# Attention and output projection on one core: stores, copies, scalings and operand loads moved where the first part ends

## The chip, the cores and the metric

The kernel runs on one core of a Trainium2 chip, in one launch. The metric is the device time of a run in microseconds (us). The engines have their own instruction queues and meet by semaphores: TensorE (PE: matrix products, transposes), VectorE (DVE), ScalarE (ACT), GpSimd (POOL), and SyncE (SP), which in this kernel issues every DMA. An instruction that has to wait holds up everything behind it in its own queue, SP's DMAs included.

## The reference

A transformer block in float32 over 8 sequences (b) of 512 rows and 1024 columns; 16 heads of 64.

```python
x = hidden                                   # [8, 512, 1024]
h = layernorm(x)
q, k, v = h @ Wq, h @ Wk, h @ Wv             # 16 heads of 64
q, k = rotary(q), rotary(k)                  # pairs of columns turned by cos, sin
s = where(causal, q @ k.T, -1e9) / sqrt(64)
attn = softmax(s) @ v
x = x + layernorm(attn @ Wo)
h = layernorm(x)
y = h @ weight.T + bias                      # plus a LoRA product chosen per sequence
x = x + layernorm(y + lora)
```

## The kernel before, in words

**Products.** All large products (values, queries and keys, output projection `wo`, feed-forward `wf`) are done by a two-level scheme in the manner of Strassen and Winograd: seven products in place of eight, and again seven in each. Operands are sums and differences called S1 to S4 and T1 to T4 beside the blocks L11 ... R22. So a unit of work is 7 groups (P1 to P7) of 7 products, 49 "ticks" (`N2`), and one tick on PE is one product: for queries and keys 8 matrix instructions, for the projection 4.

**The clock of the program.** There is no planner with costs. The order of the work is written by hand: `at(tick, fn)` puts a function on a tick, and `run(tick, filler)` first emits what is marked "pe" on that tick, then the tick's product, then everything else on it in the order in which it was registered. Each engine's queue, SP's too, has its instructions in this order and takes them strictly one after the other. A number such as 57 in the code is therefore not a time but a place in the queues.

**First part.** Values of all sequences come first (not touched here). Then eight units u = 0 to 7 (`UQ` = 8) each make queries and keys of half of the heads for two sequences. A product's two operands, `ls` and `xs`, are loaded eight products ahead into a ring of nine (`load_slot`). The results stand in tiles A, B, D, E, F; `plan_unit` says on which ticks the sums are made and the rotation (`rotate`, six steps) is done: for each half j of the tokens and half q of the heads, steps 0 to 3 are multiplications on VectorE, step 4 two additions on GpSimd or VectorE, and step 5 stores the rotated rows to the `qk` tiles by 8 DMAs, from SBUF to SBUF (lines 681 to 689).

**Attention** over unit u is done beside the products of unit u + 1, in eight pairs (`Pair`: two heads of one sequence; pairs 2i and 2i + 1 share the heads i). A pair handles its four blocks of 128 rows as (0, 1), (2) and (3):

- `scores`: PE makes s in PSUM (line 742). One tile of s exists; the next scores wait until VectorE has read it.
- `exps`: VectorE adds the mask and takes the smallest value (line 763), ScalarE exponentiates (line 773) and sums.
- `scale`: VectorE's reciprocal (line 781), then ScalarE multiplies each row (line 784).
- `transpose`: PE turns the blocks (line 798) into PSUM tiles `ptp`, of which two exist.
- `keep`: the turned blocks are copied to `pT` in SBUF (lines 808, 809 and 812), the first head (j = 0) by ScalarE and the second (j = 1) by VectorE; in the last unit both copies of block 2 are VectorE's.
- `values`: PE multiplies by v into `po` (line 818); `store` copies that to `ops` (VectorE, line 833), and after the last pair of a sequence `sum` makes the differences on GpSimd and stores them to `attn` in DRAM (lines 846, 848 and 849).

The pairs of unit 6 run beside unit 7, one in 5 ticks. Those of unit 7 have no unit beside them ("alone"): they are planned 6 ticks apart from tick 51 of unit 7, and run on into ticks 2 to 59 of a further unit "8" that has no products. From its tick 20 on PE fills with the first 21 products of the output projection of sequence 0 (`first_product`; groups P1, P2, P4), one in three ticks and later one a tick.

**Second part.** The projection of sequences 0 to 7 and then their feed-forward, 49 products each, go on from the 22nd product (`AHEAD` = 21; from here ticks count from 0 at sequence 0, so sequence 1 begins at tick 49). `plan_right(q, base)` plans for item q the loads of R11, R21, R12 and R22 from `attn` and GpSimd's differences T1 = R12 - R11, T2 = R22 - T1, T4 = R21 - T2, T3 = R22 - R12 (`sum_right`, line 275). Item q's operands are put in buffers that item q - 1 has done with: `next_roles` says which; R12 goes where T4 was, R22 where T1 was. Left operands `wo_S2` and `wo_S4` are loaded by `load_sums` (line 242) into memory that the `qk` tiles and the mask leave when the last scores have been read (`rows_qk`, closed at tick 49). For q = 1 the loads are on ticks 21 (R12), 29 (R22), 30 (R11) and 33 (R21).

Of the kernel before, what the change touches and what calls it, by code (L numbers as in the profile page):

```python
# [13 lines left out]
ALU = mybir.AluOpType  # L14
# [118 lines left out]
def sandwich_kernel(  # L133
# [15 lines left out]
    nc = tc.nc  # L149
# [44 lines left out]
    def at(tick, fn, kind=None):  # L194
        events[tick].append((kind, fn) if kind else fn)
# [48 lines left out]
    def open_right(pool, q, n):  # L244
        RX[q, n] = pool.tile([P, 7, 2, P], F32, tag=f"g{role[n]}", name=f"{n}_{q}")

    def load_right(pool, q, n):

        g, h = int(n[1]) - 1, int(n[2]) - 1
        open_right(pool, q, n)  # L250
        if q < B:
            nc.sync.dma_start(out=RX[q, n], in_=attn[q][:, g, h])
            return
        src = x1t[q - B]
        nc.sync.dma_start(
            out=RX[q, n][:, 0:4].rearrange("p (t k) c n -> p t (k c n)", t=2),
            in_=src[:, 2 * h : 2 * h + 2, ts(g, NH), :].rearrange("p t k n -> p t (k n)"),
        )
# [6 lines left out]
    def sum_right(pool, q, n, eng, part=slice(0, 3)):  # L265

        x, y = {"T1": ("R12", "R11"), "T2": ("R22", "T1"), "T4": ("R21", "T2"), "T3": ("R22", "R12")}[n]
        if (q, n) in RX:
            pass
        elif n == "T3":  # L270
            RX[q, n] = RX[q, "R12"]
        else:
            open_right(pool, q, n)
        for c in (slice(0, 2), slice(2, 4), slice(4, 7))[part]:
            eng.tensor_tensor(RX[q, n][:, c], RX[q, x][:, c], RX[q, y][:, c], op=ALU.subtract)  # L275
# [77 lines left out]
    def combine(q, out, x, y, eng):  # L353
        for j in (ALL,) if eng is nc.vector else (0, 1):
            eng.tensor_tensor(C[q, out][:, j], C[q, x][:, j], C[q, y][:, j], op=ALU.add)  # L355
# [181 lines left out]
    for b in range(B):  # L537
        base = b * N2
# [46 lines left out]
    for n in range(8):  # L585
        base = min(n + 1, B - 1) * N2
# [9 lines left out]
    UQ = NG * B // 2  # L596
    PAIRS = B
# [54 lines left out]
    def add_cu(u, out, x, i, eng):  # L652
        o, x = CU[u, out][:, i], CU[u, x][:, i]
        eng.tensor_tensor(o, o, x, op=ALU.add)
# [36 lines left out]
    def plan_unit(u, base):  # L691
        dve, pool = nc.vector, nc.gpsimd
        end = u + 1 == UQ
        for k, eng, out, x in (
            (15, pool, "B", "A"), (22, pool, "A", "D"), (29, pool, "E", "A"), (36, pool, "F", "E"),
        ):
            for i in range(2):
                at(base + k, lambda out=out, x=x, i=i, eng=eng: add_cu(u, out, x, i, eng))
        for k, i, out, x in (
            (43, 0, "A", "D"), (44, 0, "D", "E"), (44, 1, "A", "D"), (45, 1, "D", "E"),  # L700
            (49 if end else 50, 0, "E", "A"), (51 if u else 52, 1, "E", "A"),
        ):
            at(base + k, lambda out=out, x=x, i=i: add_cu(u, out, x, i, dve))

        for j, q, ticks in (
            (0, 0, (38, 39, 40, 41, 42, 44)),
            (0, 1, (41, 42, 45, 46, 47, 49) if end else
                   (42, 46, 47, 48, 49, 51) if u == 0 else (46, 47, 48, 49, 50, 52)),
            (1, 0, (46, 47, 49, 49, 49, 49) if end else
                   (49, 50, 51, 53, 54, 55) if u == 0 else (52, 53, 54, 55, 56, 58)),  # L710
            (1, 1, (52, 53, 54, 55, 56, 58) if end else (57, 58, 59, 60, 61, 63)),
        ):
            eng = dve if (end or u == 0) and j and not q else pool
            for step in range(6):
                at(base + ticks[step], lambda j=j, q=q, s=step, e=eng: rotate(u, j, q, s, e))
# [3 lines left out]
    class Pair:  # L719
# [58 lines left out]
        def scale(self, qbs):  # L778
            for qb in qbs:
                rs = work2["small"].tile([P, 2], F32, tag="rs", name=f"rs_{self.name}_{qb}")  # L780
                nc.vector.reciprocal(rs, self.sm[qb])  # L781
                for j in range(2):
                    v = self.pr[qb][:, j, :]
                    nc.scalar.mul(v, v, rs[:, j : j + 1])  # L784

        def transpose(self, qbs):
            if qbs[0] == 0:
# [14 lines left out]
        def keep(self, qbs):  # L802
            for j in range(2):

                act = j == 0 and (self.u + 1 < UQ or qbs[0] != 2)
                copy = nc.scalar.copy if act else nc.vector.tensor_copy
                if qbs[0] == 0:
                    copy(self.pT[j][:, 0, 0 : 2 * P], self.pt[j][:, 0:2, :])
                    copy(self.pT[j][:, 1, P : 2 * P], self.pt[j][:, 2, :])
                else:  # L810
                    (qb,) = qbs
                    copy(self.pT[j][:, : qb + 1, ts(qb, P)], self.pt[j][:, : qb + 1, :])  # L812
# [121 lines left out]
    for u in range(UQ + 1):  # L934
        for k in () if u in (0, UQ) else (4, 13, 22, 31) if u in (4, 5, 6) else (9, 19, 29):
            base = u * N2 + k
# [17 lines left out]
    AHEAD = 3 * NP  # L954
# [28 lines left out]
    for u in range(UQ + 1):  # L983
        base = u * N2
        if u < UQ:
            plan_unit(u, base)
        if 0 < u < UQ - 1:
            for n in range(PAIRS):
                Pair(u - 1, n).plan(base + 10 + (n * N2 + PAIRS // 2) // PAIRS)
        elif u == UQ - 1:  # L990
            for n in range(PAIRS):
                Pair(u - 1, n).plan(base + 9 + 5 * n, last=11)
            for n in range(PAIRS):
                Pair(u, n).plan(base + 51 + 6 * n, alone=True)
        if u < UQ:
            for n in range(base, base + N2):
                run(n, lambda n=n: unit_product(n))
        else:
            run(base, lambda: cur.drain(NP))
            for k in range(base + 1, base + 10):  # L1000
                run(k, None)
            streams.close()
            chunks.close()

            wop, gp, cl = (tc.alloc_tile_pool(name=name, bufs=1) for name in ("w2", "g2", "cl"))
            env["cl"] = cl
            tl = tc.alloc_tile_pool(name="tl", bufs=1)
            for k, n in (
                (10, "R11"), (10, "L11"), (15, "R12"), (17, "R22"), (21, "L12"), (24, "R21"), (31, "L22"), (42, "S1"),
            ):  # L1010
                if n in ("R11", "R12", "R21", "R22"):
                    at(base + k, lambda n=n: load_right(gp, 0, n))
                else:
                    at(base + k, lambda n=n: load_sums(wop, "wo", n, n))
            for k, n in ((21, "T1"), (26, "T2"), (32, "T4"), (44, "T3")):
                for m in range(3):
                    at(base + k + m, lambda n=n, m=m: sum_right(gp, 0, n, nc.gpsimd, slice(m, m + 1)))
            at(base + 52, lambda: combine(0, "c11", "c11", "A", nc.vector))
            cur, ticks = None, [*range(20, 44, 3), *range(44, 57)]
            for k in range(10, 57):  # L1020
                if k in (54, 56):
                    n = {54: "S2", 56: "S4"}[k]
                    load_sums(wop2, "wo", n, n)
                if k == 49:
                    rows_qk.close()
                    wop2 = tc.alloc_tile_pool(name="w2b", bufs=1)
                    load_sums(wop2, "wo", "S3", "S3")
                if k in ticks:
                    run(base + k, lambda n=ticks.index(k): first_product(n))
                else:  # L1030
                    run(base + k, None)
            cur.drain(NP)
            run_rest()
# [3 lines left out]
    with ExitStack() as a:  # L1037
# [92 lines left out]

        def plan_right(q, base):

            at(max(base + 6, AHEAD), next_roles)
            for n, k in (("R11", 10), ("R21", 17), ("R12", 24), ("R22", 31)):
                if q == 1:
                    k = AHEAD + {"R12": 0, "R22": 8, "R11": 9, "R21": 12}[n]
                at(base + k, lambda n=n: load_right(gp, q, n))
                if q >= B:
                    at(base + k + 4, lambda n=n: sub_right(q, n, nc.gpsimd))
            for n, k in (("T1", 44 if q == 1 else 38), ("T2", 45), ("T4", 52), ("T3", 63)):  # L1140
                eng = nc.vector if q >= B and n in ("T1", "T3") else nc.gpsimd
                for m in range(3):
                    at(
                        base + k + (m if eng is nc.vector else 0),
                        lambda n=n, m=m, eng=eng: sum_right(gp, q, n, eng, slice(m, m + 1)),
                    )
# [76 lines left out]
        for q in range(NQ):  # L1223
            base = q * N2
            if q + 1 < NQ:
                plan_right(q + 1, base)
            if q >= B - 1 and q + 1 < NQ:
                k = 10 if q == B - 1 else 52
# [115 lines left out]
```

## Time and profile before

| | us |
|---|---|
| median of 3 runs | 2520.49 (2519.02 to 2520.89) |
| the profiled execution | 2516.67 |
| its span, first to last instruction | 2514.9 |

| engine | busy, share of the span | instructions |
|---|---|---|
| PE, products | 2399.3 us, 95% | 12192 |
| DVE | 1745.5 us, 69% | 3842 |
| ACT | 1096.5 us, 44% | 2748 |
| POOL | 1508.8 us, 60% | 1127 |

The mean granted clock of TensorE was 0.986 of full. Times inside the profile are in us from the first instruction. A line of the timeline gives start, length, engine (a q behind it: only the issue, as of a DMA), the line of the kernel, the operation, output<-inputs, and in brackets how long the engine had been idle and who ended that. In lists of waits the numbers are total us, how many, and the longest. The page's rows of digits cut the span into 40 slices; a digit is the busy share in tenths. How the stretch from 1540 to 1760 us looks in windows of 20 us:

| window, us | PE busy | DVE busy | ACT busy | POOL busy | clock | what runs |
|---|---|---|---|---|---|---|
| 1540 to 1560 | 19.01 | 17.79 | 10.84 | 6.59 | 1.00 | end of unit 7 |
| 1560 to 1580 | 17.90 | 19.45 | 12.07 | 7.82 | 1.00 | its last products, pairs 5 to 7 of unit 6 |
| 1580 to 1600 | 9.93 | 15.32 | 7.40 | 4.75 | 0.75 | change to the pairs of unit 7 |
| 1600 to 1620 | 16.64 | 13.50 | 16.86 | 9.69 | 0.91 | pairs alone |
| 1640 to 1660 | 16.88 | 14.24 | 16.80 | 12.93 | 1.00 | pairs alone, some projection products |
| 1700 to 1720 | 20.00 | 8.54 | 2.23 | 7.56 | 1.00 | projection of sequence 0 |
| 1720 to 1740 | 15.76 | 11.00 | 5.14 | 17.16 | 0.91 | start of sequence 1 |
| 1740 to 1760 | 19.73 | 16.08 | 12.71 | 15.48 | 1.00 | sequence 1 |

### The profile page before, as it was taken

What the parts mean: (1) busy time and instruction counts of PE and PEld (TensorE: products, weight loads), DVE (VectorE), ACT (ScalarE), POOL (GpSimd) and SP (SyncE); (2) the same over time, 40 slices, a digit from 0 to 9 for tenths busy, and PEclk for the clock granted to TensorE, in tenths of its full rate; (3) what the DMA queues carried; (4) which work ended last, traced back from release to release, by engine and by line L of the source; (5) the groups of instructions that cost most, each with busy time, mean ns of one, the idle gap of its engine ahead of it and who ended that gap; (6) DMA issues with size and microseconds to landing.
All of it is one profiled execution on the core that took longest, in us unless ns stands there. A gap on an engine that the chain in (4) does not pass through costs nothing. (4 is left out here: it accounts for less than half of the span.)

```text
span 2514.9 us, 37116 instructions
## 1 busy us (share of the span) xinstructions
PE 2399.3 (95%) x12192; PEld 1882.0 (75%) x12192; DVE 1745.5 (69%) x3842; ACT 1096.5 (44%) x2748; POOL 1508.8 (60%) x1127
## 2 busy tenths in 40 slices
PE   6999999989999999999999999789999999999997
PEld 4887887777777777777777766457888887888886
DVE  8777766284957759486785957765677776766676
ACT  3323321015555556555555655673444544222222
POOL 3878875225363554637466263336777686887875
PEclk8999999999999999999999999899999999999999
DMA  7687788899899898989989895557656677334434
GB/s 259 205 288 258 246 264 266 285 287 274 265 305 276 257 332 255 328 268 299 322 266 328 255 313 175 183 178 269 207 185 203 218 275 258 133 125 145 141 105 139
DMA packets 415666, 606.02 MB, mean 241 GB/s; under 512 B 127889, under 2 KB 243601, under 8 KB 410866
## 3 DMA queue, kind: packets, MB, share of 16 engines
q1 hardware_dynamic: 415474, 603.64, 73.5%
q8 instruction: 99, 1.62, 0.3%
q14 instruction: 93, 0.76, 0.1%
HBM read 368.65 MB, written 201.33 MB: 227 GB/s over the span
## 5 line engine op out<-in xcount | busy, mean ns | idle before, releaser
L773 ACT ACTIVATE pr<-pr,nm 128x128 f32<-128x128 f32 (+3 forms) x512 | 280.8, 550 | 176.6 <-DVE nm L763 176.4
L784 ACT ACTIVATE pr<-pr,rs 128x128 f32<-128x128 f32 (+3 forms) x512 | 251.8, 551 | 117.7 <-DVE rs L781 117.7
L763 DVE CUSTOM_DVE_ANT_0 pr<-s,mask 128x128 f32<-128x128 f32 (+3 forms) x512 | 224.2, 484 | 40.2 <-PE s L742 37.6
L636 PE MATMUL accb_q_P<-xs,ls 128*128 128x256 f32 x896 | 218.1, 387 | 6.9 <-DVE u_q_P L116 6.9
L636 PE MATMUL accc_q_P<-xs,ls 128*128 128x256 f32 x896 | 218.8, 387 | 4.7 <-DVE E_q L116 4.7
L636 PE MATMUL acca_q_P<-xs,ls 128*128 128x256 f32 x896 | 220.2, 389 | 0.8 <-issue 0.8
L1091 POOL TENSOR_TENSOR c<-c,row 128x512 f32<-128x512 f32 x120 | 160.8, 1360 | 88.2 <-ACT c L415 79.2
L636 PEld LDWEIGHTS acca_q_P<-xs,ls 128*128 128x128 f32 x896 | 167.4, 192 | 52.1 <-issue 22.7
L636 PEld LDWEIGHTS accc_q_P<-xs,ls 128*128 128x128 f32 x896 | 166.3, 191 | 52.7 <-issue 21.7
L636 PEld LDWEIGHTS accb_q_P<-xs,ls 128*128 128x128 f32 x896 | 166.4, 191 | 51.0 <-DVE u_q_P L116 7.7
L742 PE MATMUL s<-qk 64*128 64x128 f32 (+3 forms) x1024 | 192.0, 471 | 7.2 <-DVE nm L763 5.1
L275 POOL TENSOR_TENSOR T<-R,T 128x512 f32<-128x512 f32 (+1 forms) x96 | 173.1, 1829 | 38.1 <-PE accc_P L315 22.7
L798 PE MATMUL ptp<-ident,pr 128*128 128x128 f32 x1280 | 177.6, 277 | 8.4 <-ACT pr L784 7.3
L798 PEld LDWEIGHTS ptp<-ident,pr 128*128 128x128 f32 x1280 | 147.3, 142 | 39.6 <-ACT pr L784 14.2
L562 POOL TENSOR_TENSOR wc_g<-wc_g 128x256 f32<-128x256 f32 (+1 forms) x120 | 122.9, 1042 | 90.1 <-DMA wc_g<-in_wqk_dram 74.7
L818 PE MATMUL po<-pT,v 128*64 128x384 f32 (+3 forms) x1024 | 155.9, 443 | 13.7 <-ACT pT L812 9.8
L677 POOL TENSOR_TENSOR B_q<-B_q,m 128x1024 f32<-128x1024 f32 x16 | 39.7, 2479 | 213.0 <-DVE B_q L675 213.0
L818 PEld LDWEIGHTS po<-pT,v 128*64 128x64 f32 x1024 | 69.7, 138 | 107.2 <-issue 67.0
L337 DVE TENSOR_TENSOR p_P<-accb_P,p_P 128x256 f32<-128x256 f32 x109 | 45.0, 413 | 101.4 <-PE accb_P L315 52.5
L812 DVE COPY pT<-ptp 128x512 f32<-128x512 f32 (+1 forms) x136 | 82.8, 614 | 42.0 <-PE ptp L798 42.0
L337 DVE TENSOR_TENSOR u_P<-accb_P,p_P 128x256 f32<-128x256 f32 x109 | 46.1, 423 | 94.6 <-ACT p_P L342 94.5
L636 PE MATMUL accd_q_P<-xs,ls 128*128 128x256 f32 x448 | 108.9, 386 | 1.1 <-ACT E_q L125 0.7
(1104 smaller groups left out, 5813.0 us busy)
## 6 DMA issues: line engine op xcount, KB each, us to landing
ls<-wqk SPq DMA_DIRECT2D x392, 256.0 KB, 4.9
xs<-xop SPq DMA_DIRECT2D x392, 256.0 KB, 5.1
R<-attn SPq DMA_DIRECT2D x32, 896.0 KB, 5.5
wqk<-wc_g SPq DMA_DIRECT2D x16, 1568.0 KB, 9.4
x<-in_x_dram SPq DMA_DIRECT2D x32, 512.0 KB, 9.7
v<-vd SPq DMA_DIRECT2D x64, 256.0 KB, 4.9
attn<-ops SPq DMA_DIRECT2D x16, 1024.0 KB, 8.3
row<-in_x_dram SPq DMA_DIRECT2D x32, 512.0 KB, 5.7
```

What stands on the lines that cost most here:

```text
L275: eng.tensor_tensor(RX[q, n][:, c], RX[q, x][:, c], RX[q, y][:, c], op=ALU.subtract)
L337: add = lambda out, x, a: nc.vector.tensor_tensor(out, acc[a], x, op=ALU.add)
L562: eng.tensor_tensor(out, x, y, op=op)
L636: nc.tensor.matmul(acc[:, :, w, :], lhsT=ls[:, k, w, :], rhs=xs_[:, :, k, :], start=(first and w == 0 and k == 0), stop=True, skip_group_c ...
L742: nc.tensor.matmul(ps[:, j, at : at + L], lhsT=qT[r, qb], rhs=kT[r, : qb + 1], start=True, stop=True,)
L763: nc.vector.tensor_tensor_reduce(out=v[:, j, :], in0=self.ps[qb][:, j, :], in1=work2["mask"][:, S - L :], scale=-1.0 / HD**0.5, scalar=3.0e38,
L773: nc.scalar.activation(v[:, j, :], v[:, j, :], AF.Exp, bias=nm[:, j : j + 1], scale=-1.0, accum_out=sm[:, j : j + 1],)
L784: nc.scalar.mul(v, v, rs[:, j : j + 1])
L798: nc.tensor.transpose(pt[:, n, :], self.pr[qb][:, j, ts(kb, P)], ident)
L812: copy(self.pT[j][:, : qb + 1, ts(qb, P)], self.pt[j][:, : qb + 1, :])
L818: nc.tensor.matmul(po[j * HD : (j + 1) * HD, kb * P :], lhsT=self.v[:, kb, ts(j, HD)], rhs=self.pT[j][:, kb, kb * P :], start=(kb == 0), s ...
L1091: nc.gpsimd.tensor_tensor(c, c, row[q, t][:, ts(h, HALF)], op=ALU.add)
```

## The change

Four edits, all near the end of the first part.

- (a) In unit 6 alone, step 5 of rotation (1, 0), its 8 row stores, is on tick 57 instead of 58.
- (b) In `keep`, n counts the pairs from the first pair of the last unit. For n = -2, -1 and 0 (the last two pairs of unit 6, the first of unit 7) ScalarE makes all copies to `pT`; elsewhere nothing changes.
- (c) In `scale`, for the last unit, heads i = 1 to 3, blocks 2 and 3 and the second head (j = 1) of the pair, VectorE multiplies in place of ScalarE: 12 instructions.
- (d) `wo` S2 is loaded at tick 51 of unit "8" instead of 54. Sequence 1's change of roles and its loads of R12, R11 and R21, in this order, are on tick 57 of unit "8", ahead of the store of the last pair's differences on tick 59. R22 is on tick 31 of the second part instead of 29, and T1 of sequence 1 on tick 40 instead of 44.

```diff
-                   (49, 50, 51, 53, 54, 55) if u == 0 else (52, 53, 54, 55, 56, 58)),
+                   (49, 50, 51, 53, 54, 55) if u == 0 else (52, 53, 54, 55, 56, 57 if u + 2 == UQ else 58)),
...
                 for j in range(2):
                     v = self.pr[qb][:, j, :]
-                    nc.scalar.mul(v, v, rs[:, j : j + 1])
+                    if self.u + 1 == UQ and self.i and qb > 1 and j:
+                        nc.vector.tensor_scalar(v, v, rs[:, 1:2], None, op0=ALU.mult)
+                    else:
+                        nc.scalar.mul(v, v, rs[:, j : j + 1])
...
-                act = j == 0 and (self.u + 1 < UQ or qbs[0] != 2)
+                n = self.u * PAIRS + 2 * self.i + self.s - (UQ - 1) * PAIRS
+                act = -2 <= n < 1 or j == 0 and (n < 0 or qbs[0] != 2)
                 copy = nc.scalar.copy if act else nc.vector.tensor_copy
...
+            at(base + 57, next_roles)
+            for n in ("R12", "R11", "R21"):
+                at(base + 57, lambda n=n: load_right(gp, 1, n))
             at(base + 52, lambda: combine(0, "c11", "c11", "A", nc.vector))
             cur, ticks = None, [*range(20, 44, 3), *range(44, 57)]
             for k in range(10, 57):
-                if k in (54, 56):
-                    n = {54: "S2", 56: "S4"}[k]
+                if k in (51, 56):
+                    n = {51: "S2", 56: "S4"}[k]
                     load_sums(wop2, "wo", n, n)
...
-            at(max(base + 6, AHEAD), next_roles)
+            if q > 1:
+                at(base + 6, next_roles)
             for n, k in (("R11", 10), ("R21", 17), ("R12", 24), ("R22", 31)):
-                if q == 1:
-                    k = AHEAD + {"R12": 0, "R22": 8, "R11": 9, "R21": 12}[n]
+                if q == 1 and n != "R22":
+                    continue
                 at(base + k, lambda n=n: load_right(gp, q, n))
...
-            for n, k in (("T1", 44 if q == 1 else 38), ("T2", 45), ("T4", 52), ("T3", 63)):
+            for n, k in (("T1", 40 if q == 1 else 38), ("T2", 45), ("T4", 52), ("T3", 63)):
```

## The prediction

> **What bounds the kernel now.** I read the page's 40 slices first, to find where TensorE (PE) is not busy.
>
> ```profile
> span 2514.9 us, 37116 instructions
> PE   6999999989999999999999999789999999999997
> DVE  8777766284957759486785957765677776766676
> PEclk8999999999999999999999999899999999999999
> ```
>
> A slice is 62.9 us. PE is full almost everywhere; the dip in slices 26 and 27 (1572 to 1698 us) is where the query/key units end and attention runs alone. The edited lines all work between 1430 and 1740 us. Next come the waits of PE alone, between 1380 and 1780 us (total us, times, longest):
>
> ```profile
> PE po L818 <- ACT pT L812: 9.8, 7, 2.6
> PE ptp L798 <- ACT pr L784: 5.2, 4, 4.0
> PE po L818 <- DVE pT L812: 3.9, 1, 3.9
> PE accb_P L315 <- DMA R<-attn: 2.3, 1, 2.3
> PE s L742 <- DMA qk<-D_q: 2.0, 2, 1.8
> PE accb_P L315 <- POOL T L275: 1.4, 1, 1.4
> ```
>
> These are three places: the start of unit 7 (`qk<-D_q`), its end (`pT`, `pr`) and the start of the output projection (`R<-attn`, `T`). Everything after them is issued in program order, with PE busy 19.5 to 20 of every 20 us from 1740 on, so a microsecond won here should reach the end. A wait costs more than itself: this is the clock in two of the windows behind such waits (busy us of each engine, then granted clock, DMA share, GB/s).
>
> ```profile
> 1450.00:1452.00 2.00, 2.00 (x6) 1.64 (x5) 0.72 (x4) 1.31 (x4) 2.00 (x2) 0.50 1.03 300
> 1724.00:1726.00 2.00, 2.00 (x6) 1.55 (x5) 0.00 (x0) 0.00 (x0) 2.00 (x3) 0.50 0.17 67
> ```
>
> The timeline gives the causes (start, length, engine; in brackets idle time and who ended it):
>
> ```profile
> 1433.48 3.34 POOL L678 TENSOR_TENSOR D_q<-D_q,m 128x1024 f32<-128x1024 f32 x1
> 1439.74 0.58 SPq L687 DMA_DIRECT2D qk<-E_q  x1
> 1447.60 0.88 PE L742 MATMUL s<-qk 64*128 64x384 f32 x2 [1.82 <-DMA qk<-D_q]
> ...
> 1581.01 0.56 ACT L812 COPY pT<-ptp 128x512 f32<-128x512 f32 x1
> 1584.71 1.22 DVE L678 TENSOR_TENSOR D_q<-D_q,m 128x1024 f32<-128x1024 f32 x1
> 1585.84 0.68 DVE L812 COPY pT<-ptp 128x512 f32<-128x512 f32 x1
> 1586.58 4.02 PE L818 MATMUL po<-pT,v 128*64 128x512 f32 x14 [3.89 <-DVE pT L812]
> ...
> 1644.48 1.49 ACT L784 ACTIVATE pr<-pr,rs 128x128 f32<-128x128 f32 x4 [0.77 <-DVE rs L781]
> 1652.84 0.56 DVE L763 CUSTOM_DVE_ANT_0 pr<-s,mask 128x384 f32<-128x384 f32 x1 [1.03 <-PE s L742]
> ...
> 1707.99 3.13 SPq L252 DMA_DIRECT2D R<-attn  x4
> 1722.84 4.25 POOL L275 TENSOR_TENSOR T<-R,R 128x512 f32<-128x512 f32 x3 [10.06 <-DMA R<-attn]
> ```
>
> First group: GpSimd (POOL) finishes the rows at 1436.8, their stores are issued only from 1439.7. Second: ScalarE (ACT) has copied its half of `pT` by 1581.6, the other half stands behind VectorE's (DVE's) rotation until 1585.8. Third: in the alone phase ACT waits for DVE and DVE for PE. Fourth: the operands R are issued at 1708 and GpSimd waits ten microseconds for them.
>
> **The change part by part**
>
> (a) Rows a step sooner. Unit 6 issues the 8 stores of rotation (1,0) at tick 57 instead of 58. On SP they then stand ahead of one product's two operand loads (issued 1438.2 and 1438.6) and of the 0.61 us issue of a weight chunk (1439.0), and can go when POOL ends, at 1436.8: 2.9 us sooner. The fourth store, which closes the first pair's rows, was issued at 1441.65 and waited on until 1448.6; 2.9 sooner is 1445.7, just where PE ends its product (1445.8). Both waits (1.82 + 0.18) go. The half clock row behind them lasts about 3.4 us (0.50 at 1450 to 1452, 0.65 to 1454), in which PE is busy: 1.7 more. Sum 3.7. SP now waits at these stores for POOL's last 0.4 us or so; behind it stand operand loads issued eight products ahead, some 24 us at 3.03 us a product (1186 us for 392), so nobody waits. The weight chunk comes some 3 us later; POOL, which sums it, idled 8.6 us just before it. Ends: 1.0 (DMA share was 1.02 to 1.03 around 1448 to 1452, and rows land late anyway) and 4.0.
>
> [...]
>
> (b) Copies on ScalarE. For the last two pairs of unit 6 and the first of unit 7 all `pT` copies go to ACT: 4 + 4 + 5 = 13 copies move. Three spots count. One: the 0.54 us copy of 1576.3 leaves DVE, so the rotation ends at 1585.3, not 1585.9. Two: the copy of 1585.84 runs on ACT right behind that of 1581.01, done by 1582.1; PE's values, which with wait and half clock ended at 1590.6, end near 1584.5 (2.37 us at full clock). DVE's next instruction (`ops`, 1590.63) then starts at 1585.3: 5.3 sooner. Three: before the reciprocal of 1597.76, which PE's 3.99 us wait at 1598.72 hangs on, two copies (0.42 + 0.28) and one of 0.55 leave DVE; with overlap 0.9 more. So 6.2 us by 1598. What could be late next is the score matmul on the last unit's (1,0) rows: they landed at 1589.5, 0.5 sooner now, and are wanted by about 1590.8; they hold. Against it: from 1609.1 to 1617.9 ACT has no idle time (3.00 of 3 us busy in both windows from 1608), and the first pair of unit 7 adds two short copies there (0.45 back to back), two of 128x384 (0.8) ahead of the copy that PE's values wait for at 1615.35, and one of 128x512 (0.47) for their second half: 1.7 us back. Net 4.5. The other copies lie where ACT idles (it is busy 12 of 20 us until 1580) and cost nothing; without that they would be 0.4 to 0.6 each. Ends: 0 (ACT takes all back) and 6.8.
>
> (c) Scaling on VectorE. In pairs 2 to 7 (counted from 0) of the last unit one 128x384 and one 128x512 scaling go from ACT to DVE: 12 instructions. The alone phase turns in 11.04 us a pair, and its loop is: scores, DVE reduction, DVE copy of `ops`, two DVE copies, reciprocal, ACT scaling of the small blocks, ACT exponentials, ACT copy, PE values, transposes, scores. The moved scalings are not in it: ACT waits 0.77 for DVE behind one and DVE 1.03 for PE behind the other. So I count 0. The trace of before has no such multiply on DVE; nearest are the 128x512 and 128x384 copies and reductions, 0.69 and 0.55. From below, a 128x2 reciprocal took 0.15. From above, a two-input 128x1024 DVE operation took 1.22 alone and 2.43 beside POOL, so 1.38 for 128x512. I take 0.69 (same size): under the 1.03 of cover that four of the five following reductions have. At 1.38 they cost 4 x 0.35 + 1.0 at the fifth (cover 0.36) = 2.4. As a gain at most 1.
>
> [...]
>
> (d) Operands in another order. S2 is loaded at tick 51, not 54, so ahead of the attention store that SP waits on until 1693.9. The regions it takes are read last by 1680.2 (S3's load, held for the same, is issued then), and DMA idles: 0.54 share from 1680 to 1700. That takes 1.8 MB (4.8 to 5.8 us between landings there) out of a DMA queue that is full from 1694 to 1725. R12, R11 and R21 of the second item are loaded at tick 57, behind PE's last product with the buffer of R12 (1696.4), and no longer behind the last attention store (POOL's sums end 1706.4). By landings: stores 1701, S4 about 1706.5, then 2.2 each for R12, R11, R21: 1713; the last stores 1717.6, R22 (tick 31 in place of 29) 1719.8, before it was 1720.5. R11 landed near 1722.7 and held PE for 2.25, with a half clock row (3.4 us, 1.7 lost): both go. T1, at tick 40, follows the POOL sum ending 1712.8; T2 waits for R22 until 1719.8, and T2 5.25, the c21 sums 2.5 and T4 4.26 end at 1731.8. PE asks for T4 at 1739.03 - 1.44 - 3.95 = 1733.6: that wait of 1.44 goes too, with 1.8 us to spare. Sum 5.4. Behind T2 on POOL stand only sums that now come earlier. Ends: 2.25 (T2 late by another R22) and 6.0 (also the 0.55 at 1735.6).
>
> **Sum.** 3.7 + 4.5 + 0 + 5.4 = 13.6 off the profiled span of 2514.9, so 2501.3. That execution took 2516.67, 1.8 more than its span, and the median of the runs is 3.8 above it: 2501.3 + 1.8 + 3.8 = 2506.9.
>
> **The rivals**
>
> ScalarE takes back what VectorE gives: the 13 copies queue behind exponentials and (b) is worth 0. For it: ACT's full windows from 1608; against: its idle time before 1600. 2511.4.
>
> The half clock stays: other waits in the same 3.4 us keep it. (a) is 2.0, (d) 3.7, sum 10.2: 2510.3. For it: halves of 6.8 us around 1583 and 1597 came with several waits each; against: both single rows follow one wait. [...]
>
> The moves do not do what they say: rows land no sooner on a full DMA (1.0), R22 holds T2 (2.25), copies 0, multiplies cost 2.4: 0.9 gained, 2519.6. For it: shares over 1.0 in both spots; against: POOL is done 2.9 us before the stores.
>
> Slower: the multiplies enter the loop. If each takes the worst DVE row beside POOL, 2.43 for either size, a pair grows by 4.86 - 1.03, six pairs by 23: 2529.9. It decides at 13.6/6 + 1.03 = 3.3 us for both together. For it: POOL runs operand sums for much of 1634 to 1655; against: half the size of the row, and reductions of 0.69 keep 0.69 beside POOL.
>
> **How the numbers follow.** Forecast 0.50, ScalarE 0.20, half clock 0.12, moves void 0.10, slower 0.08. A measurement of this kernel tells about 0.2%, 5 us, from no change. Faster is the first three, 0.82; same 0.10; slower 0.08. The forecast's own range is 2503 to 2510. The range is 2502.5 (every part at its upper end: 4.0 + 6.8 + 1.0 + 6.0 = 17.8) to 2515.5 (5.0 won: (a) whole, (d) at its low end of 2.25, a third of (b), multiplies at 1.38, so 3.7 + 2.25 + 1.5 - 2.4); it leaves out the last two cases, 0.18.
>
> **What would show it.** (a): stores issued near 1437, no PE wait on `qk<-D_q`, clock 1.00 behind it. (b): no `po` wait on DVE; if ACT takes it back, `po` waits on ACT grow at the first pair of unit 7. (c): still about 11 us a pair, multiplies under 1.03. (d): R issued near 1696, no PE wait on `R<-attn` or `T`. Wrong if the multiplies are long, or if a later wait, such as PE's 3.12 us at 2078, grows by what was won.

## The result, and the profile after

The changed kernel took 2504.94 us in the median of 4 runs (2503.67 to 2509.09), the kernel before 2519.76 (2518.46 to 2520.89) in 4 runs beside it: a ratio of 0.9942, interval 0.9929 to 0.9954. It is faster by 14.8 us; 2506.9 was forecast, with 2502.5 to 2515.5 as the range. The profiled execution of the changed kernel took 2504.95, its span 2503.2.

The page's slices first, those of the kernel after:

```profile
span 2503.2 us, 37098 instructions
PE   6999998989999999999999999899999999999997
DVE  8777766284857759586684856775777777766676
PEclk8999999999999999999999999899999999999999
```

The dip of PE was two slices wide, a 7 and an 8; it is now one 8 wide. The waits of PE alone between 1380 and 1780 us, kernel after (total us, times, longest; line numbers are 3 to 4 higher than before, so L822 is the old L818, L816 the old L812 and L801 the old L798):

```profile
PE po L822 <- ACT pT L816: 9.8, 7, 2.6
PE s L742 <- DVE nm L763: 4.8, 8, 1.9
PE ptp L801 <- ACT pr L787: 4.1, 4, 1.6
PE ptp L801 <- ACT pT L813: 1.1, 1, 1.1
PE accb_P L315 <- POOL T L275: 0.6, 1, 0.6
...
PE s L742 <- DMA qk<-D_q: 0.4, 1, 0.4
```

The 3.9 us on VectorE's `pT` and the 2.3 us on `R` are gone, the 2.0 on `qk` have become 0.4, the 1.4 on `T` 0.6, the longest on `pr` has gone from 4.0 to 1.6. The 9.8 us on ScalarE's `pT`, which no part of the change aimed at, are the same to the tenth. The windows behind the old waits, and one that is new, kernel after (columns as in the prediction's fence):

```profile
1450.00:1452.00 2.00, 2.00 (x14) 1.80 (x13) 2.00 (x6) 0.47 (x1) 1.18 (x2) 1.00 0.99 343
...
1618.00:1620.00 2.00, 1.28 (x4) 0.45 (x6) 0.77 (x6) 2.00 (x9) 0.00 (x0) 0.72 1.05 420
1620.00:1622.00 2.00, 2.00 (x8) 0.73 (x6) 0.00 (x0) 0.94 (x4) 0.00 (x0) 0.50 1.02 415
...
1724.00:1726.00 2.00, 2.00 (x11) 1.77 (x10) 0.72 (x4) 1.52 (x2) 2.00 (x3) 1.00 0.74 165
```

At 1450 and 1724 the clock is 1.00 where it was 0.50. At 1618 to 1622 it is 0.72 and 0.50: a half-clock stretch of 3.4 us that the kernel before did not have. The timeline of the kernel after, at the places that the prediction showed:

```profile
1438.76 0.52 SPq L687 DMA_DIRECT2D qk<-E_q  x1
...
1578.61 1.04 ACT L816 COPY pT<-ptp 128x512 f32<-128x512 f32 x2
1579.23 2.85 PE L822 MATMUL po<-pT,v 128*64 128x512 f32 x16 [2.61 <-ACT pT L816]
1583.91 0.68 DVE L837 COPY ops<-po 128x512 f32<-128x512 f32 x1
1585.37 1.05 PE L801 MATMUL ptp<-ident,pr 128*128 128x128 f32 x6 [1.64 <-ACT pr L787]
...
1618.72 4.07 PE L822 MATMUL po<-pT,v 128*64 128x512 f32 x16 [1.21 <-ACT pT L816]
...
1690.79 3.16 SPq L252 DMA_DIRECT2D R<-attn  x3
1714.52 6.33 POOL L275 TENSOR_TENSOR T<-R,T 128x512 f32<-128x512 f32 x3 [3.11 <-DMA R<-attn]
1727.59 1.13 PE L315 MATMUL accb_P<-wo_L,T 128*128 128x256 f32 x4 [0.62 <-POOL T L275]
```

ScalarE now makes both copies of `pT` at 1578.61 in one go, and VectorE's `ops`, which stood at 1590.63, comes at 1583.91 (1.9 us of this lead were there before the stretch). The operands are issued at 1690.79 in place of 1707.99 (5.6 of it won before). GpSimd still waits 3.11 us for the last of them, and PE still 0.62 us for T.

**Where the time went.** To put a price on each part, the same instruction is sought in two traces, and the change of the distance between two of them is taken, so that whatever an execution has lost or won earlier drops out. The marks, by their times in the profile of before: VectorE's copies to `ops` at 1443.29, 1567.72, 1605.51, 1631.45 and 1696.74, and ScalarE's copies to p at 1462.52, 1716.19 and 1734.73. Each number is how much longer (+) or shorter (-) the stretch is than in that profile. The third column averages over the executions that lack the edit, that of before among them as 0 (it and those of the experiments below), because some stretches differ from one execution of unchanged code to the next; the fourth over those that have it.

| part, stretch | changed kernel | without the edit: mean (lowest to highest) | with it: mean (lowest to highest) | worth, with less without | predicted |
|---|---|---|---|---|---|
| (a) 1443 to 1462 | -4.60 | -0.87 (-2.31 to +1.31), 7 | -4.60 (all), 7 | -3.7 | -3.7 |
| (b) 1568 to 1606 | -6.54 | +0.87 (0 to +2.11), 7 | -5.42 (-6.84 to -4.12), 7 | -6.3 | -6.2 |
| (b) 1606 to 1631 | +3.34 | +0.05 (-0.04 to +0.34), 10 | +3.35 (+3.34 to +3.35), 4 | +3.3 | +1.7 |
| (c) 1631 to 1697 | -0.46 | 0.00 (0.00 to +0.01), 7 | -0.52 (-0.55 to -0.46), 4 | -0.5 | 0 |
| (d) 1716 to 1735 | -5.84 | +0.31 (0 to +0.55), 5 | -5.64 (-5.84 to -5.34), 7 | -6.0 | -5.4 |

The second column adds up to -14.1, the fifth to -13.2, the prediction's terms to -13.6. (The two profiled spans differ by 11.7 only: that of the changed kernel had lost 2.65 by 1443 us, before any edited instruction, and -14.1 + 2.65 - 0.3 after 1735 is -11.7. The 0.3 and the 2.65 are the scatter of single executions.)

### The profile page after: what moved, and what is told of

Read it like the earlier page. It is cut to its first block, busy times and chain, and to the rows that moved or that the text cites. A ratio compares the mean times of both kernels' runs of the same rounds, so it can differ in the third digit from the quotient of the medians.

```text
span 2503.2 us, 37098 instructions
## 1 busy us (share of the span) xinstructions
PE 2397.0 (96%) x12192; PEld 1882.0 (75%) x12192; DVE 1742.4 (70%) x3841; ACT 1093.9 (44%) x2749; POOL 1511.9 (60%) x1127
## 5 line engine op out<-in xcount | busy, mean ns | idle before, releaser
L787 ACT ACTIVATE pr<-pr,rs 128x128 f32<-128x128 f32 (+2 forms) x500 | 245.1, 548 | 113.8 <-DVE rs L781 113.7
L801 PE MATMUL ptp<-ident,pr 128*128 128x128 f32 x1280 | 177.6, 277 | 6.6 <-ACT pr L787 5.3
L801 PEld LDWEIGHTS ptp<-ident,pr 128*128 128x128 f32 x1280 | 147.4, 142 | 38.3 <-ACT pr L787 12.3
L822 PE MATMUL po<-pT,v 128*64 128x384 f32 (+3 forms) x1024 | 156.8, 443 | 9.8 <-ACT pT L816 9.8
L822 PEld LDWEIGHTS po<-pT,v 128*64 128x64 f32 x1024 | 71.4, 138 | 102.5 <-issue 65.1
L742 PEld LDWEIGHTS s<-qk 64*128 64x128 f32 x1024 | 72.8, 186 | 46.1 <-issue 30.0
```

The lines of the kernel that those rows point to most:

```text
L742: nc.tensor.matmul(ps[:, j, at : at + L], lhsT=qT[r, qb], rhs=kT[r, : qb + 1], start=True, stop=True,)
L801: nc.tensor.transpose(pt[:, n, :], self.pr[qb][:, j, ts(kb, P)], ident)
L822: nc.tensor.matmul(po[j * HD : (j + 1) * HD, kb * P :], lhsT=self.v[:, kb, ts(j, HD)], rhs=self.pT[j][:, kb, kb * P :], start=(kb == 0), s ...
```

## The experiments

The first four do one part of the change alone, all on one chip; the kernel before had a median of 2519.11 there.

**Rows alone.** Only (a):

```diff
-  (49, 50, 51, 53, 54, 55) if u == 0 else (52, 53, 54, 55, 56, 58)),
+  (49, 50, 51, 53, 54, 55) if u == 0 else (52, 53, 54, 55, 56, 57 if u + 2 == UQ else 58)),
```

> Part (a) alone. My theory: the rows of unit 6 land before PE asks, so PE's wait on qk<-D_q near 1447 us and the half clock behind it go, and PE is 3.7 to 4.6 us earlier from 1462 us on, up to the end: about 2515.5. Rival (half clock stays): only 2.0 to 2.9 earlier, 2517.3, with a half-clock stretch still near 1450. Rival (rows land no sooner): 2519.8. Everything after 1560 us is as before: the waits of 3.9 and 4.0 us on pT and pr stay.

Measured: 2516.09 (2511.34 to 2522.08), ratio 0.9989 (0.9978 to 1.0). Its stretch is 4.60 shorter, there is no wait on `qk<-D_q` near 1448 and the clock is 1.00 from 1446 to 1454. Both the wait and the half clock go, as predicted. That the runs show 3.0 and not 4.6 (the interval reaches from 0 to 5.5) fits the third column of the table: unchanged code has this boundary 0.87 shorter on average than the profile of before had it, since in three of those executions the wait was only 1.3 to 1.4 us and no half clock followed.

**Copies alone.** Only (b), in `keep`:

```diff
-  act = j == 0 and (self.u + 1 < UQ or qbs[0] != 2)
+  n = self.u * PAIRS + 2 * self.i + self.s - (UQ - 1) * PAIRS
+  act = -2 <= n < 1 or j == 0 and (n < 0 or qbs[0] != 2)
```

> Part (b) alone. My theory: po no longer waits on VectorE; the ops copy of the last pair of unit 6 is 6.2 to 6.6 us earlier against before, the one after the first pair of unit 7 gives back 1.2 to 1.7 of it (ScalarE full), net 4.5 to 4.9, about 2515.2. If in the changed kernel a further 1.7 was lost by a half-clock stretch near 1619 us, that is chance of where the window falls and need not appear here. Rival (ScalarE takes all back): 2519.8, with the ops copy of the second pair of unit 7 no earlier than before.

Measured: 2516.28 (2510.84 to 2523.67), ratio 0.9985 (0.9972 to 0.9998). 6.47 won by 1606, then 1.65 and 1.70 given back, so 3.1 stay. The 1.65 is the term of the prediction; the 1.70 is a half-clock stretch at 1624.51, the same one as in the changed kernel, and so comes with this part.

**Scaling alone.** Only (c), in `scale`:

```diff
-  nc.scalar.mul(v, v, rs[:, j : j + 1])
+  if self.u + 1 == UQ and self.i and qb > 1 and j:
+      nc.vector.tensor_scalar(v, v, rs[:, 1:2], None, op0=ALU.mult)
+  else:
+      nc.scalar.mul(v, v, rs[:, j : j + 1])
```

> Part (c) alone. My theory: 0 (within 0.5): the pairs of unit 7 still turn in 11.0 us each, the multiplies take 0.35 to 0.69 and lie in VectorE's idle time; 2519.8. Rival (the multiplies enter the loop): each pair from the third on longer by 0.3 to 3.8, 2521 to 2530. Rival (ScalarE is the bound of the alone phase and is relieved): shorter by up to 1.2 a pair, 2512.

Measured: 2519.88 (2517.11 to 2524.12), ratio 0.9999 (0.999 to 1.0009). The pairs keep their turn of 11.04; 0.55 is won, once, between the sixth and seventh. This part alone cannot be told from no change in the time. The multiplies themselves, in the changed kernel (min/median/max ns):

```profile
L785 DVE TENSOR_SCALAR pr<-pr,rs x12: 420/486/1164, 1617.2 to 1681.3; 128x384 f32<-128x384 f32 x6, 128x512 f32<-128x512 f32 x6
```

**Operands alone.** Only (d): S2 at tick 51; R12, R11, R21 at tick 57 of unit "8", R22 at 31, T1 at 40.

```diff
+ at(base + 57, next_roles)
+ for n in ("R12", "R11", "R21"):
+     at(base + 57, lambda n=n: load_right(gp, 1, n))
...
- n = {54: "S2", 56: "S4"}[k]
+ n = {51: "S2", 56: "S4"}[k]
...
- (("T1", 44 if q == 1 else 38), ...
+ (("T1", 40 if q == 1 else 38), ...
```

> Part (d) alone. My theory: the waits on R<-attn (2.25) and on T (1.44) and the half clock behind the first go; PE is 5.4 to 5.9 us earlier from 1760 us on, 2514.2; nothing changes before 1690 us. Rival (R22 holds T2): 2.25 only, 2517.5, with a wait on POOL's T of over 1.4. Rival (half clock stays): 3.7, 2516.

Measured: 2511.2 (2505.71 to 2519.49), ratio 0.9969 (0.9956 to 0.9981), 5.84 won at its place and kept to the end; PE waits 0.64 for T. The largest part, and the only one of the four that shows in the time with an interval far from 1.

The next four run on another chip (before: 2519.29).

**Without the first pair of unit 7.** The changed kernel with n = 0 left out of (b):

```diff
- act = -2 <= n < 1 or j == 0 and (n < 0 or qbs[0] != 2)
+ act = -2 <= n < 0 or j == 0 and (n < 0 or qbs[0] != 2)
```

> The changed kernel, but the first pair of unit 7 copies as before (condition -2 <= n < 0): five copies stay on VectorE. My theory: ScalarE, full there, no longer carries 1.7 us more, so the ops copy of the first pair of unit 7 comes 1.2 to 1.7 us earlier against the changed kernel, and that stays to the end: about 2503.3 where the changed kernel has 2504.9. The half-clock stretch near 1619 us may go as well (another 1.7, 2501.6) if it comes from how the waits fall in the clock's windows. Rival (the copies on ScalarE are worth their place because VectorE is the bound there): 0 to 2 us slower than the changed kernel, 2505 to 2507.

**The changed kernel again**, beside it:

> The changed kernel once more, beside the run without the first pair's copies, for a comparison on the same chip. My theory: 2504.9, with the same gains at the same places (4.6 after unit 6's rows, 6.5 by the last pair of unit 6, 1.65 given back, 5.8 at the projection), and a half-clock stretch near 1619 us only if the waits there fall into one window again. Rival (that stretch belongs to the kernel): it is there again.

Measured: 2501.88 (2498.99 to 2506.4), ratio 0.9932 (0.9917 to 0.9947), without the first pair; 2506.36 (2504.54 to 2513.96), ratio 0.9952 (0.9935 to 0.997), as changed. The two intervals overlap a little; the medians lie 4.5 apart. What decides is the trace: between 1606 and 1631 the first gives back 0.00, the second 3.34. The values of the second pair of unit 7 in the first of the two kernels:

```profile
1617.02 0.93 PE L742 MATMUL s<-qk 64*128 64x128 f32 x8 [0.62 <-DVE nm L763]
1619.15 2.37 PE L822 MATMUL po<-pT,v 128*64 128x512 f32 x16 [1.21 <-ACT pT L816]
```

They take 2.37 us against 4.07 in the changed kernel, behind exactly the same two waits, 0.62 and 1.21; the profile of before has these two waits too:

```profile
1623.42 0.93 PE L742 MATMUL s<-qk 64*128 64x128 f32 x8 [0.62 <-DVE nm L763]
1625.55 2.38 PE L818 MATMUL po<-pT,v 128*64 128x512 f32 x16 [1.21 <-ACT pT L812]
```

So the waits are not new: what is new is where they fall between the instants at which the clock changes. Half-clock stretches in these traces are 3.41 us long or a multiple of it, the last of a profile aside, which runs past its end; and in each of the 14 profiles the changes of the granted clock lie on one grid of 3.413 us, to within 5 ns. In what follows a window is one step of that grid. Counting windows of 3.41 on from the end of the last half-clock stretch, the changed kernel has both waits, 1.83 us, in one window. Without the first pair a boundary falls at 1617.8, between them; in the profile of before at 1624.1, also between them. In the operands-alone run 1.6 of the 1.83 us fall in one window, and the clock stays full. All four executions with the first pair's copies on ScalarE have the half-clock stretch, and none of the ten without. That the windows come to lie alike all four times was seen, why they do was not shown.

**S2 alone.** Of (d), only the load of S2 at tick 51:

```diff
- n = {54: "S2", 56: "S4"}[k]
+ n = {51: "S2", 56: "S4"}[k]
```

> Of part (d) only the load of S2 at tick 51. My theory: DMA before the projection is emptied by 1.8 MB, R11 lands 4 to 5 us sooner and the wait of 2.25 us on R<-attn goes; T1, still on tick 44, starts 4 us sooner, and the wait on T shrinks or goes: 2.5 to 5.8 us gained at the start of sequence 1. Rival (the order of R's loads does it all): 0 to 1.

**R alone.** Of (d), all but that:

```diff
+ at(base + 57, next_roles)
+ for n in ("R12", "R11", "R21"):
+     at(base + 57, lambda n=n: load_right(gp, 1, n))
...
- (("T1", 44 if q == 1 else 38), ...
+ (("T1", 40 if q == 1 else 38), ...
```

> Of part (d) all but the load of S2: next_roles and R12, R11, R21 at tick 57, R22 at 31, T1 at 40. My theory: R11 lands ahead of the last attention store, about 1718, so the wait on R<-attn and its half clock go; but R22 comes as late as before or later (1725), T2 waits for it, and the wait on T stays or grows: 2.5 to 4.5 gained. Rival (S2 gives nothing): 5.8 gained as with the whole of (d).

Measured, one run each: 2514.71 and 2514.99; at their place 1.84 and 2.46 won. Neither half gives the 5.6 of both, and the two together only 4.3. Each takes away the wait on R and its half clock (4.0 by the mark at 1726, ScalarE's next copy to p after 1716.19), and each then gives back 2.2 or 1.6 at one and the same new wait, here in the run with S2 alone (VectorE, ScalarE, PE, and PE again):

```profile
1730.69 0.69 DVE L395 BATCH_NORM_STATS2 bn_o<-c 128x6 f32<-128x512 f32 x1 [3.65 <-POOL c L355]
1731.66 0.29 ACT L403 ACTIVATE sd_o<-mv_o,eps 128x1 f32<-128x1 f32 x1 [4.42 <-DVE mv_o L398]
1732.72 1.13 PE L315 MATMUL accb_P<-wo_L,R 128*128 128x256 f32 x4 [2.92 <-DVE u_P L337]
1736.16 1.13 PE L315 MATMUL accb_P<-wo_L,T 128*128 128x256 f32 x4 [1.44 <-POOL T L275]
```

T1 and T2 are still late on GpSimd; its sums c stand behind them (they end at 1731.9), VectorE's statistics wait for the sums, ScalarE's square root for the statistics, and in ScalarE's queue the copy of p stands behind the square root, for which `u_P` waits, and PE for that. In the profile of before this chain was hidden behind the wait on R: 0.55 of it showed.

```profile
1735.59 1.13 PE L315 MATMUL accb_P<-wo_L,R 128*128 128x256 f32 x4 [0.55 <-DVE u_P L337]
```

Only both halves together bring T1 and T2 early enough.

The last four run on a third chip (before: 2518.94).

**Rows a step later.** The kernel before, with the stores on tick 59:

```diff
-  (49, 50, 51, 53, 54, 55) if u == 0 else (52, 53, 54, 55, 56, 58)),
+  (49, 50, 51, 53, 54, 55) if u == 0 else (52, 53, 54, 55, 56, 59 if u + 2 == UQ else 58)),
```

> The kernel before with unit 6's rows (1, 0) stored at tick 59, a step later. My theory: a tick is some 3 us, so PE waits on qk<-D_q about 3 us longer (4 to 5 us in place of 1.3 to 2.0) and a half-clock stretch of 6.8 us follows: PE 3 to 5 us later from 1462 us on than before, 2523. Rival (the rows are held by the full DMA and not by their place in the queue): no longer wait, 2519.

Measured, one run: 2515.87, the stretch 0.15 shorter than in the profile of before, PE's wait 1.9 us with 3.4 us of half clock behind it. This execution runs 0.35 behind that profile here, so by the place that PE has reached the first store is issued 2.1 us later; it lands at the same place (1447.02 for 1446.99), and this run shows no cost. The prediction's reason for (a), a landing that follows the issue, falls. The issue of the weight chunk and of the first row store in this kernel:

```profile
1439.38 0.61 SPq L553 DMA_DIRECT2D wc_wf<-in_wf_dram  x1
1442.22 0.58 SPq L687 DMA_DIRECT2D qk<-E_q  x1
```

The chunk landed at 1444.29 and this store at 1447.37, 5.1 us after its issue. In the kernel before, the chunk is issued at 1439.03 and lands at 1446.55, and the first store, issued at 1439.74, lands at 1446.99: 7.2 us. In the changed kernel the store is issued at 1438.76, ahead of the chunk, and lands at 1442.29: 3.5 us. A row store of unit 7, issued at 1555.25 in the kernel before with nothing large ahead of it, took 2.3. In these three executions the rows landed just behind what stood ahead of them in the DMA queue: 0.44 after the chunk in the kernel before, 0.41 and 0.33 after an operand load (landed at 1441.88 and 1447.04) in the changed kernel and in this one.

This run, whose operand loads are those of the kernel before, also shows the chain behind the wait on R, without an edit there. No half clock followed that wait (2.35 us); PE was 1.40 ahead of the profile of before by the mark at 1726, and by 1735 it was 0.10 behind. It lost this at a wait on `u_P`, 0.55 us in the kernel before:

```profile
1736.82 1.13 PE L315 MATMUL accb_P<-wo_L,R 128*128 128x256 f32 x4 [2.24 <-DVE u_P L337]
```

**Both heads' scaling on VectorE.** The changed kernel with twice the multiplies:

```diff
- if self.u + 1 == UQ and self.i and qb > 1 and j:
-     nc.vector.tensor_scalar(v, v, rs[:, 1:2], None, op0=ALU.mult)
+ if self.u + 1 == UQ and self.i and qb > 1:
+     nc.vector.tensor_scalar(v, v, rs[:, j : j + 1], None, op0=ALU.mult)
```

> The changed kernel with both heads' scalings of blocks 2 and 3 on VectorE in pairs 2 to 7 of the last unit, so the cost under dispute doubled. My theory: VectorE's idle time ahead of the scores covers 1.03 us a pair, so two multiplies of one block, if about 0.35 to 0.7 each, just fit or cost up to 0.4 a pair: 0 to 2 us slower than the changed kernel in the alone phase, pairs of 11.0 to 11.4. Rival (multiplies stand in the loop): at least 1 us a pair, 6 or more in all.

Measured, one run: 2505.09. The stretch from 1631 to 1697 is 0.39 longer where it was 0.46 shorter, so the twelve more cost 0.9, with a single PE wait of 1.28 on VectorE at 1650.56; the longest multiply took 1.49. The four multiplies of a pair, at a median of 0.48, take 1.9 together, under the 3.3 a pair from which that rival would have decided: VectorE has room in the alone phase, and the slower rival falls.

**Block 2 on ScalarE.** The kernel without the first pair, and from the second pair of unit 7 on the first head's copy of block 2 moved to ScalarE:

```diff
- act = -2 <= n < 1 or j == 0 and (n < 0 or qbs[0] != 2)
+ act = -2 <= n < 0 or j == 0 and (n != 0 or qbs[0] != 2)
```

> The changed kernel without the first pair's copies, and in pairs 1 to 7 of the last unit the first head's copy of block 2 on ScalarE instead of VectorE. My theory of the loop (reduction, ops, two copies of block 2, reciprocal on VectorE, then ScalarE, then PE): one copy of 0.46 us less in it, and ScalarE, which waits 0.77 us there, takes it, so the alone pairs turn in 10.6 instead of 11.0: 2.5 to 3.2 us over seven pairs, about 2499. Rival (PE or ScalarE sets the period): 11.0 or longer, 2502 or slower.

**The same without (c)**, the multiplies back on ScalarE:

```diff
-  if self.u + 1 == UQ and self.i and qb > 1 and j:
-      nc.vector.tensor_scalar(v, v, rs[:, 1:2], None, op0=ALU.mult)
-  else:
-      nc.scalar.mul(v, v, rs[:, j : j + 1])
+  nc.scalar.mul(v, v, rs[:, j : j + 1])
```

> The same without part (c): all scalings back on ScalarE. My theory: ScalarE has 0.26 + 0.77 us of waits a pair, enough for the copy of 0.46 without the scalings moved, so the pairs still turn in 10.6 to 10.8; 0.5 us lost at the end of the phase as (c) alone won there; 2499.5 to 2500.5. Rival (part (c) is what makes room on ScalarE): pairs of 11.0 again, 2502 or more.

Measured: 2503.86 (2500.09 to 2506.63), ratio 0.9934 (0.9921 to 0.9947); and 2499.18 (2498.42 to 2504.43), ratio 0.9924 (0.9908 to 0.9941). The second is the best of the study, faster than the kernel before and, by 0.9924 against 0.9942 and 0.9952, than the changed kernel, though the intervals overlap a little. From 1631 to 1697 they are 1.35 and 1.86 shorter, where 0.46 to 0.55 came with the change: the copy shortens four pairs by about 0.46 each, less than I had put it at, and it needs no multiplies moved away. In the first, one of the moved multiplies took 2.03 us, in a pair that turned in 11.52 where the second has 10.58; the first missed its forecast of 2499, and three of its five runs took 2503.86 or more. In the profile of the first, 5.7 us were lost again between the marks at 1735 and 1755, 4.5 of them in one PE wait that goes back to one VectorE addition:

```profile
1726.33 6.13 DVE L355 TENSOR_TENSOR c<-c,A 128x1024 f32<-128x1024 f32 x1
```

In the second kernel the same instruction took 1.92. That this one event explains the difference of the two medians was not shown.

## Why the prediction was right, and where it was not

The time, 2504.94, lies 2.0 below the forecast and inside its range; the sum over the marks is 13.2 to 14.1 for 13.6. That the sum came so near is in part luck: (b) is worth 1.5 less than forecast, (c) and (d) together 1.1 more. Step by step:

**(a), 3.7.** Right in size: 4.60 against the profile of before, 3.7 against the mean of unchanged executions. Both the wait and the half clock went, so the rival by which the half clock stays (2.0) falls, here and for (d). Of the 4.60, 1.7 is the half clock, so the wait had cost 2.9 and not the 2.0 of its brackets; the ends of PE's instructions are modelled. (In the three executions without half clock a wait of 1.3 to 1.4 cost 2.3.) The step that failed is its reason: "2.9 sooner is 1445.7" took the landing to move with the issue. A step later left the landing where it was. With the changed kernel's 2.65 of delay at this place taken off, its first store is issued at 1436.1 (near 1437 was forecast), 3.6 sooner than before, and lands at 1439.6, 7.4 sooner. By these landings the edit works because the rows pass the weight chunk and one product's two operand loads; no run moved the chunk alone.

**(b), 4.5 = 6.2 - 1.7.** The first term, 6.3 measured, was right, with `ops` at 1585.8 (1583.91 and the 1.9 of lead) where 1585.3 was forecast. "They hold", of the rows wanted by the score matmul, was 0.43 off: PE waits that long on `qk<-D_q` at 1587.70. What came late next was mostly ScalarE's scaling, 1.64 and 1.30 us of PE on `pr`. The second term, ScalarE's full windows, was 1.65 for 1.7. The step that failed is the one left out: a slower first pair moves the waits behind it against the windows of 3.41 us, and two waits that had cost 1.83 now cost 1.70 more. So (b) is worth 3.0 and not 4.5, and the move of the first pair's copies is a loss: without it the kernel ran at 2501.88 beside 2506.36, and its trace gives back nothing there. The rival by which ScalarE takes everything back falls: with the clock's part it took 3.3 of 6.3.

**(c), 0.** Right within 0.5. The multiply of 128x512 was taken as 0.69 after the copies of `ops` and bounded by 1.38; its median was 0.49. The bound did not hold: the longest multiply took 1.16 in this profile, 1.45 in that of the changed kernel again and 2.03 in the one with block 2 on ScalarE. The copy of `ops` reads `po` in PSUM and took 0.69, the multiply reads and writes `pr` in SBUF and took 0.49, so that row was a poor neighbour for it; what makes the difference was not shown. The slower rival falls with the two scaling experiments, where the stretch moved by -0.55 and +0.39.

**(d), 5.4.** Right: 6.0. With the lead of 5.6 added, so that the times compare with the forecast's: the operands were issued at 1696.4 (1696.4 forecast), R22 landed at 1720.0 (1719.8), T2 began at 1720.1. The step that failed is "1.8 us to spare". T2 took 6.33 and not 5.25, so T4 was done at 1733.1 and not 1731.8 (why T2 took longer was not shown); and PE, freed also of the `u_P` wait that the sum had left out, asked for it at 1732.6 and not 1733.6. It waited 0.62. What the prediction did not see is that the two halves need each other, and that its waits were not independent terms: in the run with the rows a step later the half clock behind R was missing, and the chain behind took all of it back (PE 1.40 ahead at 1726 and 0.10 behind by 1735).

The rival "moves void" falls with 13 to 14 us found at their places.

## What to carry to other kernels

A wait costs what it hides as well as itself: another chain may stand right behind it, as at the operands, where either half of the edit won 4.0 us, gave back 2.2 or 1.6 at the next wait, and both were needed. The row stores here landed 0.33 to 0.44 us behind what stood ahead of them in the DMA queue, and 2.1 us later in the issue left the landing where it was, so look at what a transfer has to pass, and not at the instant of its issue alone. Relief given to one engine by another paid where the receiver was idle at that moment (6.3 us at the last pairs of unit 6); check it pair by pair, since here one pair too many cost 3.3 us.

## What the hardware showed that was not expected

- TensorE's clock. Counted over the 14 profiles from 20 to 2480 us, in windows on the grid of 3.413 us: all 97 windows at full clock with 2.0 us or more of PE idle time were followed by half clock, and so were 22 of 29 with 1.8 to 2.0, none of 17 with 1.65 to 1.8, 12 of 283 with 0.8 to 1.65, and none with less. (In the profiles of before and after alone: all 14, both of 2, none of 2, 3 of 45 and none of 1345.) From half it came back after 145 of 148 windows with under 0.65 us idle and after none of 59 with more (21 of 21 and none of 10 in those two). The idle time is that between PE's records, whose ends are modelled. Half clock lasted 3.41, 6.83 or 10.24 us in those two, the last stretch of each aside. What sets the grid, and why some windows with 0.8 to 2.0 us idle were followed by half clock and others not, was not shown.
- A VectorE operation on two 128x1024 inputs took 1.22 us alone (1584.71 in the profile of before), 2.43 (there at 1573.97) and 2.78 (1722.53 with S2 alone) beside GpSimd. In the profile of before the 132 that ran with no GpSimd instruction beside them took 1.20 to 1.23, the 123 that ran wholly beside GpSimd 1.22 to 3.37, with a median of 1.85. An addition took 6.13 once, in the first kernel with block 2 on ScalarE: GpSimd was busy until 1731.4, VectorE done at 1732.5, and GpSimd's own instructions beside it ran at their usual pace (three of 128x512 on R in 4.29 us, against 4.25 for three in the profile of before; two on c in 2.50, there 2.48). Why it took so long was not shown.
- A 128 KB row store took 7.2 us to land with a 0.5 MB chunk right ahead of it, 3.5 right behind operand loads of 0.25 MB, and 2.3 with nothing large ahead.
